# A two-layer sequence model on one core: layer 0's gelu by tanh, the last units' work split between engines, single units routed, and the plan's place

## The chip, the core and the metric

The kernel runs on one core of a Trainium2 chip. A core has five engines, each with its own queue of instructions that it takes strictly in order: TensorE (PE, with weight loads shown as PEld), VectorE (DVE), ScalarE (ACT), GpSimd (POOL) and SyncE (SP, which here only issues transfers). Engines wait for each other by semaphores. The metric is the device time of one execution in microseconds (us). Line numbers (L748) are those of the kernel before.

## The reference, cut to what matters

The input x has 8 sequences of 1024 tokens with 256 features. Two layers follow, each with a post-norm.

```python
# layer 0: feature-wise linear attention, then gelu (the tanh form), then a spectral filter
Q = elu(x@Wq + bq) + 1;  K = elu(x@Wk + bk) + 1;  v = x@Wv + bv
V = Q * sum(K*v, 1) / (Q * sum(K, 1) + 1e-6)
x = layernorm(x + gelu(V@Wo + bo))                  # jax.nn.gelu, approximate
x = layernorm(x + real(ifft(fft(x) @ w)) + bias)
# layer 1: causal softmax attention with 16 heads and a linear position bias
x = layernorm(x + attention(x))
# ... then a block whose attention runs ACROSS the 8 sequences at each position,
#     and a mixture of 8 experts, top 2, 2560 places for each expert
h = x + attn_over_sequences(ln(x)) @ proj.T
p = softmax(ln(h) @ router);  top2 = top_k(p, 2)
# rows of an expert are numbered in token order; rows past its capacity are dropped
moe[token] += gelu_exact(rows @ w1[e]) @ w2[e] * weight
x = layernorm(x + h + moe)
```

## The kernel before, in words

A sequence n is worked through in four steps.

*Layer 0* (`pre(n)`): the sequence is loaded, transposed, multiplied by the three weights, and comes through elu, sums, a reciprocal and the output product. `added` (L725) ends a half layer for four blocks of two tiles each (128 x 512 values): PE's product in PSUM, the bias added by DVE (`shifted`, L736), for the first half the gelu on ACT (L748) and the addition to x on POOL (L753). The blocks' tiles come from a ring of two buffers (`half_row`); elu's tiles from a ring of five (`row`). ACT's functions need tables; those of Exp and of the gelu by tanh are different ones, and a change loads a table.

*Softmax attention* (`run`, L1672 on): for each sequence and each of four head groups 24 steps. A step makes the scores of one piece for the weights (L938, mask L949) with ACT's exponential into `pT` (L952), the scores of the next head group for its row maxima (L872, mask L882) with DVE's maximum (L885), and the value products of an earlier piece (L965). There is one PSUM buffer for each of the two kinds of scores.

*Across sequences* (`across`): in units of two tiles (256 positions, u = 0 to 3 in each sequence), norm, projection, DVE's products of queries and keys (L1223) and their sums over a head (L1239), softmax over the sequences so far (L1255 to L1276), POOL's weighing of the values (`weigh`, L1289, two instructions for each part of two sequences), for the last two sequences gathered by PE (L1338), projection and sum (L1397, L1409), second norm (DVE statistics, POOL root L1079 and L1082, ACT), router product and copy `rt` (L1447).

*Routing* (`dispatch`, L1453 on): for half a sequence, two units at once: softmax, top 2, the rank of each row in its expert (PE L1521 and L1524, DVE L1531), its place, and four fields beside each row (POOL L1599, L1606); then one indirect transfer for each tile and each of the two choices sends 128 rows into the expert-sorted buffer `xg` (L1617): four sends for a unit.

The order of instructions is written out when the kernel is built. Work beside attention is made of tasks, each with an engine and a cost; a planner keeps a clock for each engine, and between the steps it issues those tasks that fit ahead of the next scores (`beside`), or, without attention beside them, the one that can start first (`drain`). `pre(n+2)` is queued in the last head group of sequence n, `across(n-1)` in the first of sequence n. So a changed cost or a changed task may change the order of everything behind it. For the last sequence (n = 7) attention goes by halves of the queries; its units 2 and 3 come after the last attention, with more ring buffers.

Behind that stands the *plan* (L1862 on): DVE computes from the counts of the eight experts which block of 256 rows belongs to which expert, and the indices of the rows to fetch. Then come the *experts*: rows are fetched by POOL's indirect transfers (L2006), run through both products (L2056, gelu L2063, L2070), weighed, normed and put into the output (L2120).

## Time and profile before

| what | value |
|---|---|
| median of 3 runs | 3421.26 us (3418.32 to 3422.33) |
| profiled execution, its own time | 3418.51 us |
| its span, first to last instruction | 3416.8 us |
| PE busy | 3158.0 us (92%) |
| DVE busy | 2163.0 us (63%) |
| ACT busy | 1403.1 us (41%) |
| POOL busy | 1323.3 us (39%) |
| first and last exponential of L952 | about 167 and 2359 us |
| first fetch for the experts (L2006) | 2470.65 us |

The page cuts the span in 40 slices and gives each engine's busy share in tenths. A group's row tells line, engine, operation, output from input, shapes, count, then the busy time, the mean of one in ns, the idle time of the engine just before these instructions and what ended most of it. A row of the stage windows tells the stretch, its length, and for each engine its busy time with the number of instructions, then PE's granted clock, the DMA share and GB/s. A timeline's row tells start, duration, engine, line, operation, and in brackets the idle time before it and what ended it. PE's ends are modelled, so a busy PE need not be PE at its peak.

### The profile page before, as it was taken

The page shows a single profiled execution, that of the slowest core. Times are in us where ns is not written, and L with a number is a line of the kernel's source. Part 1 is how long each engine was busy: PE and PEld are TensorE (multiplying, and loading weights), DVE is VectorE, ACT ScalarE, POOL GpSimd, SP SyncE. Part 2 cuts the span into 40 slices and gives each one's busy share as a digit, 9 for nine tenths or more (in the row PEclk, how much of TensorE's full clock was granted, in tenths as well). Part 3 has the DMA queues.
Part 4 walks back from the last instruction along what each step waited for, and adds up shares of the span by engine and source line. Part 5 has one row for each costly group of instructions (what it writes and reads, how often), then busy time and mean ns, then how long its engine had stood idle before and what let it go on. Part 6 is the DMA issues. An engine that isn't in the chain of part 4 may idle for free. (4 is left out here: it accounts for less than half of the span.)

```text
span 3416.8 us, 51611 instructions
## 1 busy us (share of the span) xinstructions
PE 3158.0 (92%) x19664; PEld 1880.7 (55%) x19664; DVE 2163.0 (63%) x5125; ACT 1403.1 (41%) x2314; POOL 1323.3 (39%) x1671
## 2 busy tenths in 40 slices
PE   6899999999999999998989988998399999999998
PEld 4434435444445434444444434455388888888887
DVE  5666576776776786688688678887534433343443
ACT  3245456565556556456546544444011111111111
POOL 3111012221322222223232323447556666666665
PEclk9999999999999999999999999999699999999999
DMA  2085000010110110111111111232314425334231
GB/s 87 1 155 111 1 21 27 29 35 4 56 44 17 52 40 17 52 40 38 50 35 38 40 50 55 67 118 83 126 55 138 137 63 187 91 112 137 90 116 49
DMA packets 142957, 227.23 MB, mean 67 GB/s; under 512 B 25290, under 2 KB 114452, under 8 KB 139760
## 3 DMA queue, kind: packets, MB, share of 16 engines
q1 hardware_dynamic: 104640, 114.87, 11.9%
q0 software_dynamic: 37248, 108.22, 9.9%
q8 instruction: 156, 2.56, 0.3%
q14 instruction: 97, 0.79, 0.1%
q10 hardware_dynamic: 816, 0.79, 0.1%
HBM read 232.08 MB, written 94.19 MB: 95 GB/s over the span
## 5 line engine op out<-in xcount | busy, mean ns | idle before, releaser
L885 DVE TENSOR_REDUCE mx<-s 128x2 f32<-128x1024 f32 (+3 forms) x768 | 733.5, 955 | 402.6 <-PE s L882 270.8
L952 ACT ACTIVATE pT<-st 128x1024 f32<-128x1024 f32 (+3 forms) x768 | 622.6, 811 | 717.2 <-PE st L949 475.3
L938 PE MATMUL st<-qt,kt 32*128 32x512 f32 (+3 forms) x3072 | 715.7, 542 | 125.1 <-ACT pT L952 115.5
L872 PE MATMUL s<-kt,qt 32*128 32x512 f32 (+3 forms) x3072 | 714.8, 542 | 7.1 <-DVE mx L885 6.1
L938 PEld LDWEIGHTS st<-qt,kt 32*128 32x128 f32 x3072 | 233.6, 186 | 497.3 <-ACT pT L952 351.7
L2063 ACT ACTIVATE hT<-h 128x512 f32<-128x512 f32 x256 | 152.8, 597 | 761.3 <-PE h L2056 761.3
L2056 PE MATMUL h<-xeT,we 128*128 128x256 f32 x2048 | 454.5, 380 | 1.4 <-DVE xeT L1991 1.4
L2070 PE MATMUL y<-we,hT 128*128 128x256 f32 x2048 | 452.5, 379 | 0.0
L2070 PEld LDWEIGHTS y<-we,hT 128*128 128x128 f32 x2048 | 389.1, 190 | 52.9
L2056 PEld LDWEIGHTS h<-xeT,we 128*128 128x128 f32 x2048 | 385.2, 191 | 51.7 <-DVE xeT L1991 1.8
L2090 DVE SCALAR_TENSOR_TENSOR yo<-y,ws,sums 128x256 f32<-128x256 f32 x128 | 61.7, 482 | 464.5 <-DMA sums<-out,row 334.2
L965 PE MATMUL pv<-pT,vv 128*32 128x512 f32 (+3 forms) x3072 | 332.3, 505 | 0.5 <-ACT pT L952 0.5
L872 PEld LDWEIGHTS s<-kt,qt 32*128 32x128 f32 x3072 | 233.2, 185 | 39.4 <-DVE mx L885 33.3
L1005 POOL TENSOR_TENSOR x<-x,ah 128x256 f32<-128x256 f32 x64 | 49.4, 772 | 433.7 <-DVE ah L994 384.6
L1289 POOL TENSOR_TENSOR pa<-v,sc 128x256 f32<-128x256 f32 (+1 forms) x266 | 159.3, 628 | 128.2 <-DVE sc L1276 65.1
L949 PEld LDWEIGHTS <-late_keys 128*128 128x128 bf16 x1024 | 58.3, 97 | 229.2 <-issue 214.2
L2120 POOL DMA_INDIRECT out<-yo,row x128 | 135.0, 1054 | 68.7 <-DVE yo L2111 47.5
L2006 POOL DMA_INDIRECT xin<-xg,idx_x x128 | 134.7, 1053 | 41.3 <-issue 26.2
L949 PE MATMUL st<-ident_h,late_keys 128*128 128x128 bf16 x1024 | 147.3, 226 | 0.0
L1617 POOL DMA_INDIRECT xg<-h,id x128 | 132.5, 1035 | 37.5 <-issue 33.0
L2038 POOL DMA_INDIRECT sums<-out,row x128 | 130.0, 1016 | 43.1 <-issue 38.0
L882 PE MATMUL s<-late_keys,ident_h 128*128 128x128 bf16 x1024 | 143.1, 222 | 0.0
(257 smaller groups left out, 4697.5 us busy)
## 6 DMA issues: line engine op xcount, KB each, us to landing
xg<-zero SPq DMA_DIRECT2D x8, 2610.0 KB, 28.4
x<-in_x SPq DMA_DIRECT2D x8, 1024.0 KB, 13.9
lone<-total SPq DMA_DIRECT2D x64, 128.0 KB, 2.4
xmid<-x SPq DMA_DIRECT2D x6, 1024.0 KB, 4.4
xh<-xmid SPq DMA_DIRECT2D x24, 256.0 KB, 2.7
out<-xh SPq DMA_DIRECT2D x24, 256.0 KB, 2.1
total<-xh SPq DMA_DIRECT2D x24, 256.0 KB, 2.4
we<-in_wexp SPq DMA_DIRECT2D x3, 2048.0 KB, 15.2
```

Of the source, the lines that this page charges most:

```text
L872: nc.tensor.matmul(ps[:, u, :kn], lhsT=qt[r0 : r0 + 32, i * P : (i + 1) * P], rhs=kt[r0 : r0 + 32, k0 : k0 + kn], start=True, stop=not diag,)
L882: nc.tensor.matmul(ps[:, u, kn - P : kn], lhsT=ident_h, rhs=late_keys, start=False, stop=True)
L885: nc.vector.tensor_reduce(out=mxs[g % 2][:, i, 2 * pair : 2 * pair + 2, half], in_=ps[:, :, :kn], axis=AX.X, op=ALU.max,)
L938: nc.tensor.matmul(st[:, u, :w], lhsT=kt[r0 : r0 + 32, kb * P : (kb + 1) * P], rhs=qt[r0 : r0 + 32, q0 + off : q0 + 512], start=True, stop ...
L949: nc.tensor.matmul(st[:, u, :P], lhsT=late_keys, rhs=ident_h, start=False, stop=True)
L952: nc.scalar.activation(pT[:, :, :w], st[:, :, :w], AF.Exp)
L965: nc.tensor.matmul(pv[32 * hh : 32 * hh + 32, off:512], lhsT=vv[:, kb, (4 * g + hh) * VE : (4 * g + hh) * VE + 32], rhs=tiles[hh // 2][:, ...
L1289: nc.gpsimd.tensor_tensor(out=out[:, :, r * P : (r + 1) * P].rearrange("p t (g d) -> p t g d", d=HD), in0=tile[:, t0 : t0 + m, :].rearrang ...
L2056: nc.tensor.matmul(ps[:, f * GS : (f + 1) * GS], lhsT=w1_s[:, c, (f0 + f) * P : (f0 + f + 1) * P], rhs=xeT[:, c, :], start=(c == 0), stop= ...
L2063: nc.scalar.activation(hT[:, f0 : f0 + 2, :], ps.rearrange("p (f g) -> p f g", f=2), AF.Gelu)
L2070: nc.tensor.matmul(ps[:, t * D : (t + 1) * D], lhsT=hT[:, f, t * P : (t + 1) * P], rhs=w2_s[:, f, :], start=(f == 0), stop=(f == FC - 1),)
L2120: put = nc.gpsimd.indirect_dma_start(out=rows_out, out_offset=bass.IndirectOffsetOnAxis(ap=row[:, 1, i : i + 1] if i < GB else idx_l[:, b ...
```

## The change

1. Layer 0's gelu is written out: with g half of the shifted value (the output bias is halved once at the start), ACT makes the square with a scale, DVE (square + c) * g, ACT the tanh of that, DVE (tanh + 1) * g. The tile e comes from the ring of five. The gelu instruction and its table go.
2. For the last sequence's units 2 and 3, the four key products of the unit's second tile are issued on POOL. For unit 3, the weighing of its first tile is issued on DVE.
3. These two units are routed one at a time, each as soon as its router product is there (`lone`), on 2 tiles in place of 4.
4. In the routing the top-2 weights are computed ahead of the ranks, and only the field of the last choice stays behind the places.
5. The plan's block is marked to keep its written order on DVE.

```diff
+ROOT, CUBE = (2 / 3.141592653589793) ** 0.5, 0.044715
...
+    nc.vector.tensor_scalar(out=bo_r, in0=bo_r, scalar1=0.5, scalar2=None, op0=ALU.mult)
...
-                    t = Task("DVE", 0.69, shifted, [t])
-                    ps.readers.append(t)
                     if gelu:
-                        def act(g=g):
-                            nc.scalar.activation(g.get(), g.get(), AF.Gelu_apprx_tanh)
-
-                        t = Task("ACT", 0.65, act, [t], table="gelu")
+                        t = Task("DVE", 0.74, halved, [t])
+                        ps.readers.append(t)
+                        e = row.take(f"{name}e{n}_{j0}")
...
+                        t = Task("ACT", 0.6, square, [t], [e])
+                        t = Task("DVE", 0.72, inner_, [t])
+                        t = Task("ACT", 0.6, tanh, [t], table="exp")
+                        t = Task("DVE", 0.72, outer, [t])
+                        e.readers.append(t)
+                    else:
+                        t = Task("DVE", 0.69, shifted, [t])
+                        ps.readers.append(t)
...
+                        aside = n == N - 1 and u >= 2 and i == 1
...
-                            nc.vector.tensor_tensor(
+                            (nc.gpsimd if aside else nc.vector).tensor_tensor(
                                 out=pr.get()[:, :m, :].rearrange("p t (r e) -> p t r e", r=2),
...
+                        both_do = n == N - 1 and u == 3 and i == 0
...
+                        if both_do:
+                            t = late("DVE", 0.3 + 0.4 * m, part, [shared, *there], [pa])
+                        else:
+                            t = late("POOL", 0.3 + 0.5 * m, part, [shared, *there, *turn_], [pa])
+                            turn_ = [t]
...
-                if u % 2 == 0:
+                lone = n == N - 1 and u >= NB // 2 - 2
+                lo = 0 if lone else 2 * (u % 2)
+                if lo == 0:
                     rt = rtr.take(f"rt{nm}")
...
-                if u % 2:
-                    dispatch(n, u // 2, rt, routed[u // 2])
+                if lone or lo:
+                    dispatch(n, first_block, rt, routed[first_block])
...
             chosen = late("DVE", 1.25, earlier, [t])
...
+            weighed_ = late("DVE", 0.75, weights_, [chosen])
...
-            t = late("DVE", 1.5, weights_, [slots])
+            t = late("DVE", 0.8, which_last, [slots, weighed_])
...
-    with tc.tile_pool(name="plan", bufs=1) as rt:
+    with tc.tile_pool(name="plan", bufs=1) as rt, tc.manual_schedule(engines={nc.vector.engine}):
```

More of the change, by code (lines that the diff above doesn't have):

```diff
@@ L733, in added, with halved @@
                     t = token_tasks(ps, j0 % 4, use[j0 // 4], weight, need, (g,))
+                    def halved(ps=ps, g=g):
+                        nc.vector.scalar_tensor_tensor(
+                            out=g.get().rearrange("p (j d) -> p j d", d=D),
+                            in0=ps.get().rearrange("p (j d) -> p j d", d=D),
+                            scalar=0.5,
+                            in1=bias.unsqueeze(1).to_broadcast([P, 2, D]),
+                            op0=ALU.mult,
+                            op1=ALU.add,
+                        )
                     def shifted(ps=ps, g=g):
@@ L741, in shifted, with square, inner_, tanh @@
                         )
-                    t = Task("DVE", 0.69, shifted, [t])
-                    ps.readers.append(t)
                     if gelu:
-                        def act(g=g):
-                            nc.scalar.activation(g.get(), g.get(), AF.Gelu_apprx_tanh)
-                        t = Task("ACT", 0.65, act, [t], table="gelu")
+                        t = Task("DVE", 0.74, halved, [t])
+                        ps.readers.append(t)
+                        e = row.take(f"{name}e{n}_{j0}")
+                        def square(e=e, g=g):
+                            nc.scalar.activation(
+                                e.get(), g.get(), AF.Square, scale=(8 * ROOT * CUBE) ** 0.5
+                            )
+                        def inner_(e=e, g=g):
+                            nc.vector.scalar_tensor_tensor(
+                                out=e.get(),
+                                in0=e.get(),
+                                scalar=2 * ROOT,
+                                in1=g.get(),
+                                op0=ALU.add,
+                                op1=ALU.mult,
+                            )
+                        def tanh(e=e):
+                            nc.scalar.activation(e.get(), e.get(), AF.Tanh)
+                        def outer(e=e, g=g):
+                            nc.vector.scalar_tensor_tensor(
+                                out=g.get(),
+                                in0=e.get(),
+                                scalar=1.0,
+                                in1=g.get(),
+                                op0=ALU.add,
+                                op1=ALU.mult,
+                            )
+                        t = Task("ACT", 0.6, square, [t], [e])
[6 more added lines that the diff above has]
+                        ps.readers.append(t)
                     def plus(g=g, j0=j0):
@@ L1220, in across, with product @@
                         pr = prr.take(f"pr{nm}_{i}_{t0}")
-                        def product(pr=pr, tile=kv[0], qa=qa, i=i, t0=t0, m=m):
-                            nc.vector.tensor_tensor(
+                        aside = n == N - 1 and u >= 2 and i == 1
+                        def product(pr=pr, tile=kv[0], qa=qa, i=i, t0=t0, m=m, aside=aside):
+                            (nc.gpsimd if aside else nc.vector).tensor_tensor(
                                 out=pr.get()[:, :m, :].rearrange("p t (r e) -> p t r e", r=2),
@@ L1233, in product @@
                             )
-                        t = late("DVE", 0.2 + 0.27 * m, product, there[0] + got, [pr])
+                        t = late(
+                            "POOL" if aside else "DVE",
+                            0.1 + 0.58 * m if aside else 0.2 + 0.27 * m,
+                            product,
+                            there[0] + got,
+                            [pr],
+                        )
                         kv[0].readers.append(t)
@@ L1284, in across, with weigh @@
                 mx.readers.append(shared)
-                def weigh(out, tile, sc, i, t0, m):
+                def weigh(out, tile, sc, i, t0, m, engine=nc.gpsimd):
                     for r in range(2):
-                        nc.gpsimd.tensor_tensor(
+                        engine.tensor_tensor(
                             out=out[:, :, r * P : (r + 1) * P].rearrange(
@@ L1323, in across, with part @@
                         pa = par.take(f"pa{nm}_{i}_{t0}")
-                        def part(pa=pa, tile=tile, sc=sc, i=i, t0=t0, m=m):
-                            weigh(pa.get()[:, :m, :], tile.get(), sc.get(), i, t0, m)
-                        t = late("POOL", 0.3 + 0.5 * m, part, [shared, *there, *turn_], [pa])
-                        turn_ = [t]
+                        both_do = n == N - 1 and u == 3 and i == 0
+                        def part(pa=pa, tile=tile, sc=sc, i=i, t0=t0, m=m, both_do=both_do):
+                            engine = nc.vector if both_do else nc.gpsimd
+                            weigh(pa.get()[:, :m, :], tile.get(), sc.get(), i, t0, m, engine)
+                        if both_do:
[3 more added lines that the diff above has]
+                            turn_ = [t]
                         tile.readers.append(t)
@@ L1444, in across, with out @@
                 rT.readers.append(t)
-                def out(ps=ps, rt=rt, u=u):
+                def out(ps=ps, rt=rt, lo=lo):
                     nc.scalar.copy(
-                        out=rt.get()[:, 0, 2 * (u % 2) : 2 * (u % 2) + 2, :],
+                        out=rt.get()[:, 0, lo : lo + 2, :],
                         in_=ps.get()[:, : 2 * E].rearrange("p (i e) -> p i e", e=E),
@@ L1453, in across, with dispatch @@
                 ps.readers.append(t)
-                routed.setdefault(u // 2, []).append((h, t, normed))
-                if u % 2:
-                    dispatch(n, u // 2, rt, routed[u // 2])
+                first_block = j0 - lo
+                routed.setdefault(first_block, []).append((h, t, normed))
+                if lone or lo:
+                    dispatch(n, first_block, rt, routed[first_block])
         counted = []
-        def dispatch(n, hf, rt, units):
-            nm = f"{n}_{hf}"
+        def dispatch(n, first_block, rt, units):
+            nm, many = f"{n}_{first_block}", 2 * len(units)
             rs, ids = rsr.take(f"rs{nm}"), idr.take(f"id{nm}")
-            part = lambda k: rt.get()[:, k]
-            col = lambda k: rs.get()[:, k]
-            bc = lambda k: col(k).unsqueeze(2).to_broadcast([P, HB, E])
+            part = lambda k: rt.get()[:, k, :many]
+            col = lambda k: rs.get()[:, k, :many]
+            bc = lambda k: col(k).unsqueeze(2).to_broadcast([P, many, E])
             tt = nc.vector.tensor_tensor
@@ L1486, in dispatch @@
             t = late("DVE", 0.65, probs, [t])
-            each = iota_e.unsqueeze(1).to_broadcast([P, HB, E])
+            each = iota_e.unsqueeze(1).to_broadcast([P, many, E])
             def choose(k):
@@ L1510, in earlier @@
                 nc.vector.tensor_copy(out=part(4)[:, :2], in_=part(5)[:, :2])
-                tt(out=part(4)[:, 2:], in0=part(5)[:, 2:], in1=part(5)[:, :-2], op=ALU.add)
+                if many > 2:
+                    tt(out=part(4)[:, 2:], in0=part(5)[:, 2:], in1=part(5)[:, :-2], op=ALU.add)
                 tt(out=part(5), in0=part(4), in1=part(3), op=ALU.subtract)
@@ L1516, in dispatch, with weights_ @@
             flat = lambda k: part(k).rearrange("p j e -> p (j e)")
+            def weights_():
+                tt(out=col(0), in0=col(1), in1=col(2), op=ALU.add)
+                nc.vector.reciprocal(out=col(0), in_=col(0))
+                for k in range(2):
+                    tt(out=col(1 + k), in0=col(1 + k), in1=col(0), op=ALU.mult)
+            weighed_ = late("DVE", 0.75, weights_, [chosen])
             def rank():
-                n_ = HB * E
+                n_ = many * E
                 for lhs, rhs, start in ((before, 3, True), (ones, 5, False)):
@@ L1524, in rank @@
                 nc.tensor.matmul(
-                    ps.get()[:, n_ : n_ + E], lhsT=ones, rhs=part(4)[:, HB - 1], start=True, stop=True
+                    ps.get()[:, n_ : n_ + E], lhsT=ones, rhs=part(4)[:, many - 1], start=True, stop=True
                 )
@@ L1532, in ranked @@
                     out=part(5),
-                    in0=ps.get()[:, : HB * E].rearrange("p (j e) -> p j e", e=E),
-                    in1=counts.unsqueeze(1).to_broadcast([P, HB, E]),
+                    in0=ps.get()[:, : many * E].rearrange("p (j e) -> p j e", e=E),
+                    in1=counts.unsqueeze(1).to_broadcast([P, many, E]),
                     op=ALU.add,
                 )
-                tt(out=counts, in0=counts, in1=ps.get()[:, HB * E : (HB + 1) * E], op=ALU.add)
+                tt(out=counts, in0=counts, in1=ps.get()[:, many * E : (many + 1) * E], op=ALU.add)
             t = first_in("DVE", 0.4, ranked, [t])
@@ L1559, in slot @@
                 nc.vector.scalar_tensor_tensor(
-                    out=ids.get()[:, k],
+                    out=ids.get()[:, k, :many],
                     in0=col(6),
@@ L1570, in dispatch, with which_last @@
             slots = late("DVE", 1.2, lambda: slot(1), [t])
-            def weights_():
-                tt(out=col(0), in0=col(1), in1=col(2), op=ALU.add)
-                nc.vector.reciprocal(out=col(0), in_=col(0))
-                for k in range(2):
-                    tt(out=col(1 + k), in0=col(1 + k), in1=col(0), op=ALU.mult)
+            def which_last():
                 nc.vector.tensor_scalar(
@@ L1583, in weights_ @@
                 nc.vector.tensor_scalar(
-                    out=placed[:, n * NB + HB * hf : n * NB + HB * (hf + 1)],
+                    out=placed[:, n * NB + first_block : n * NB + first_block + many],
                     in0=col(7),
@@ L1596, in fields @@
                 def fields(v=v, h=h):
-                    j0 = HB * hf + 2 * v
+                    j0 = first_block + 2 * v
                     r = h.get()
```

## The prediction

> **What bounds the kernel now.** I read the page's slices first, then stage sums, then groups, then the timeline behind the last attention. The slices (each 85.4 us):

> ```profile
> PE   6899999999999999998989988998399999999998
> ...
> DVE  5666576776776786688688678887534433343443
> ...
> POOL 3111012221322222223232323447556666666665
> ```

> PE is the busy engine everywhere but in two places: the first slices, where layer 0 of the first sequence has nothing beside it, and the slice with the 3 (2392 to 2477), where attention is over and the last units of the second layer are finished one after the other. So the kernel has four stages: start (to 167, the first exponential of L952), attention with filler (to 2360), the hole (to 2471, the first row fetch of L2006), experts (to the end). The change leaves the experts' instructions as they are, so I price the other three. In the attention stage:

> ```profile
> 1000.00:1400.00 400.00, 379.15 (x2688) 180.11 (x2680) 293.15 (x593) 225.98 (x362) 108.39 (x147) 0.98 0.09 29
> ...
> sum 1460.00, PE 1382.03 PEld 635.16 DVE 1071.58 ACT 808.03 POOL 371.68; mean PE 345.51 PEld 158.79 DVE 267.89 ACT 202.01 POOL 92.92
> ```

> Over 340 to 1800 PE is idle for 1460 - 1382 = 78 us (5.3%), DVE is 73% busy, ACT 55%. What PE waits for, from the groups:

> ```profile
> L938 PE MATMUL st<-qt,kt 32*128 32x512 f32 (+3 forms) x3072 | 715.7, 542 | 125.1 <-ACT pT L952 115.5
> L872 PE MATMUL s<-kt,qt 32*128 32x512 f32 (+3 forms) x3072 | 714.8, 542 | 7.1 <-DVE mx L885 6.1
> ```

> Nearly all is waiting for ACT's exponential (there is one score buffer); DVE's maxima hardly ever stop PE.

> **Gelu by tanh: what ACT gives up.**

> ```profile
> L748 ACT ACT_TABLE_LOAD x28 | 35.9, 1283 | 2.7 <-DVE og L736 1.3 <-DVE lna L480 0.9
> L952 ACT ACT_TABLE_LOAD x27 | 34.6, 1283 | 2.6 <-PE st L949 2.1
> ...
> L748 ACT ACTIVATE og<-og 128x512 f32<-128x512 f32 x32 | 20.1, 629 | 14.4 <-DVE og L736 14.0
> ```

> The page's own 58 loads are these 55 and three single ones; in the built order of the changed program two are left (the first, and the experts' Gelu). In the attention stage 54 loads go (27 pairs, 28 blocks of two tiles). A block held ACT for 2 x 1.283 + 0.629 = 3.20 us; now Square and Tanh hold it for 2 x 0.63 = 1.26, in two pieces. That is 28 x 1.94 = 54 us less on ACT, of which only what PE waited for counts. Six windows laid around the loads (46 of the 54):

> ```profile
> 752.50:775.50 23.00, 21.04 (x156) 12.24 (x160) 18.77 (x43) 20.73 (x28) 8.11 (x10) 1.00 0.04 12
> ...
> 1575.00:1608.00 33.00, 24.49 (x182) 12.09 (x178) 23.38 (x58) 24.18 (x32) 18.86 (x26) 0.90 0.06 18
> sum 164.50, PE 135.55 PEld 71.58 DVE 123.54 ACT 130.63 POOL 68.41; mean PE 22.59 PEld 11.93 DVE 20.59 ACT 21.77 POOL 11.40
> ```

> PE idles 28.95 us of 164.5. At the stage's 5.3% it would be 8.8, so 20.2 us belong to 46 loads: 0.44 each, 23.7 for 54. If the idle time shrinks in proportion to ACT's block (1.94 of 3.20), 14.4 come back; if the short pieces disturb nothing, 23.7. I take 19. Outer bounds: 0 (PE's order is limited elsewhere) and 54 (every microsecond of ACT counts).

> [...]

> **What DVE gets.** Per block the shift becomes a scaled shift (taken as 0.05 us more than the 0.68 of L736), and two three-operand instructions on 128x512 come in; the same form at L610 takes 0.68 to 0.71. So 28 x 1.43 = 40 us more in the attention stage. Bounds: 0 (the row L872: PE waited 6.1 us for maxima in the whole run) and 40 (DVE sets the pace). Between: a run of 24 steps lasts some 68 us, so a maximum comes every 2.8 us; each of 56 new instructions of 0.69 us is hit with a chance of 0.25 and then delays it by 0.35, 56 x 0.25 x 0.35 = 5. I take 5, near the row. POOL's additions come later by about 2 us a block; two sequences of lead cover that. If the lead failed, the drain before the next head group would show it. Attention: -19 + 5 = -14.

> **Start: +3.** Here the chain is bare, and the table load (58.2) stood in a wait for the queries' product, so nothing is won by dropping it. The first pair of blocks went DVE 67.51, ACT 68.23, POOL 68.94 to 70.2 and 71.26 to 72.5. Now the second scaled shift (69.83) stands ahead of the first inner product in DVE's order: square to 71.2, products to 72.0, tanh to 72.7, outer to 73.5; POOL's additions end near 74.0 and 75.3, 2.8 later. The second pair is 4.8 later, but its filter rows waited for the first half's statistics anyway. I take +3, between 0 and +6. The halving of bo_r waits for a load issued ahead of own_c's, whose scaling waits anyway.

> **The hole: -6.** DVE's and POOL's rows there:

> ```profile
> 2385.01 1.29 DVE L1223 TENSOR_TENSOR pr<-qa,k 128x512 f32<-128x512 f32 x2 [4.27 <-DMA k<-kvd]
> ...
> 2408.90 2.10 DVE L1223 TENSOR_TENSOR pr<-qa,k 128x512 f32<-128x512 f32 x2
> ...
> 2421.00 0.42 DVE L1276 TENSOR_TENSOR sc<-sc,mx 128x256 f32<-128x256 f32 x1
> ```
> ```profile
> 2405.59 6.46 POOL L1289 TENSOR_TENSOR pa<-v,sc 128x256 f32<-128x256 f32 x8 [2.63 <-issue]
> ...
> 2427.30 5.82 POOL L1289 TENSOR_TENSOR pa<-v,sc 128x256 f32<-128x256 f32 x10
> ```

> DVE works without a pause from 2385 to 2418: 16 products, 16 sums and the routing of the half before. A product takes 0.60 start to start alone (1.29 for two), 1.05 beside POOL (2.10 for two); POOL's weighing 0.58 alone (5.82 for ten), 0.81 in that mixture (6.46 for eight). So POOL and DVE don't add up on such operands. Eight products go to POOL, into its idle stretch 2392 to 2402 (1.2 each, as L1409's 1.18 for the same size): 8 x 0.6 = 4.8 off DVE. Then unit 3's 16 weighings (2421.66 to 2433.1) halve: 8 x 0.58 = 4.6 less on POOL, but the others go at about 0.85: 8 x 0.27 = 2.2 given back. Root L1079 of unit 3 (2439.17) should come 7 us earlier, at 2432.

> [...]

> From that root on the sends count:

> ```profile
> 2439.17 0.23 POOL L1079 TENSOR_SCALAR ln<-ln 128x2 f32<-128x2 f32 x1
> ...
> 2448.16 0.98 POOL L1617 DMA_INDIRECT xg<-h,id  x1 [0.30 <-issue]
> ...
> 2457.36 0.21 POOL L1606 COPY h<-rs 128x8 f32<-128x8 f32 x1 [7.93 <-DVE rs L1580]
> ...
> 2467.44 0.97 POOL L1617 DMA_INDIRECT xg<-h,id  x1 [0.30 <-issue]
> 2470.65 1.10 POOL L2006 DMA_INDIRECT xin<-xg,idx_x  x1 [2.24 <-DMA xg<-h,id]
> ```

> Before, 7 sends follow the root, POOL waits 7.93 us for the routing, 8 follow: 29.2 us to the end of the last. Routing unit 2 alone frees four of the eight, for some 35 more DVE rows of 0.2 us that run while POOL sends. But in the changed order the products stand where eight sends stood (2380.7 to 2391.5; three are left there), and 21 sends now follow the root: 1.0 + 21 x 1.275 + 1.1 for two pairs of field writes = 28.9. The wait is filled with sends, not removed. And the plan doesn't go last: the built order still threads its DVE rows (5.5 us in 2452 to 2458) between the last routing's, so unit 3's fields come near 2453, when POOL gets there too. Moving the weights' four small rows is worth 0.5. So 7 less up to 2 of waiting: -6, between 0 and -12 (no sends piled up).

> **Sum.** +3 - 14 - 6 = -17. The profiled execution took 3418.51 (span 3416.8, 1.7 around it): 3401.5. The runs' median of 3421.26 lies 2.75 higher; I forecast 3404.

> **Rivals.** (1) ACT's relief counts more: every exponential comes sooner, 40 of its 54 us return: -35 - 6 + 3, about 3383. For it: 115.5 us of waits on ACT. Against: only some 29 us lie around the loads. (2) It does little: the idle time around loads was work that PE lacked anyway, and the planner, which writes the whole order anew from its costs, spreads it elsewhere; attention 0, hole -6, start +3: 3418. For it: the 2.3 us steps are full of filler; and the plan not moving is one part that doesn't do what it says. (3) DVE takes ACT's place (slower): in the attention stage it holds 73%, now 76%, and more in runs with routing work (313 of 400 us in 1400 to 1800). If each added DVE microsecond delays a maximum in full, +40 - 19 + 3 - 6 = +18: 3439. It is slower by over 0.2% once the price passes (6.8 + 22) / 40 = 0.72 a microsecond. Against: L872's 6.1 us.

> **Numbers.** Forecast 0.60, (1) 0.10, (2) 0.17, (3) 0.13. A new order of some 670 steps also moves things by several us either way. The range leaves out (3) and the far part of (1): 3386 to 3424. About 0.2% (6.8 us) is what a measurement here can tell: faster 0.70, same 0.17, slower 0.13.

> **What would show it.** Two table loads; in the six gelu regions PE idle near 8%, not 17%; idle before the weights' score matmuls (L938 of before) down by about 20 us, before the maxima's (L872) still under 15; first exponential near 170; hole (last exponential to first row fetch) 105 instead of 111 us, with POOL sending without a pause after the last root. Wrong if DVE's maxima become what ends PE's waits, if the last attention ends no earlier than 2350, or if POOL waits for the routing again.

## The result and the profile after

The changed kernel takes 3394.46 us (median of 6 runs, 3383.54 to 3405.03); the kernel before takes 3421.7 beside it. The ratio is 0.9926, 95% interval 0.991 to 0.9943. The profiled execution took 3396.47 us, its span is 3394.8. Lines are from here on those of the changed kernel: weights' scores L986, maxima's scores L920, exponential L1000, the gelu L764 to L782, cross-sequence products L1274 and their sums L1296, POOL's weighing L1346, root L1127, field writes L1672 and L1679, sends L1690, first row fetch L2079.

Two groups of the page of the changed kernel answer to L938 and L872 of before (busy us, mean ns, then the idle time ahead of them and what ended most of it):

```profile
L986 PE MATMUL st<-qt,kt 32*128 32x512 f32 (+3 forms) x3072 | 714.2, 541 | 110.4 <-ACT pT L1000 100.6
L920 PE MATMUL s<-kt,qt 32*128 32x512 f32 (+3 forms) x3072 | 712.2, 540 | 7.6 <-DVE mx L933 6.8
```

Waiting for ACT's exponential went from 115.5 to 100.6 us (all idle time ahead of that group from 125.1 to 110.4); the maxima still hold PE for under 8 us, with 49 us more work on DVE (2211.9 in all). Windows around the gelus of the attention stage (busy us of each engine with the number of instructions, PE's granted clock, DMA share, GB/s), laid where each kernel has its gelus, first seven of the kernel before, then nine of the changed one:

```profile
527.00:546.00 19.00, 15.74 (x114) 9.06 (x112) 13.87 (x34) 17.04 (x23) 8.87 (x13) 1.00 0.03 8
...
1579.00:1600.00 21.00, 13.55 (x124) 7.90 (x124) 17.57 (x50) 17.12 (x20) 12.21 (x18) 0.95 0.02 8
...
sum 170.00, PE 137.74 PEld 77.42 DVE 135.22 ACT 142.67 POOL 66.85; mean PE 19.68 PEld 11.06 DVE 19.32 ACT 20.38 POOL 9.55
```
```profile
535.00:561.00 26.00, 26.00 (x172) 13.65 (x174) 22.56 (x46) 16.96 (x32) 8.63 (x9) 1.00 0.26 81
...
1560.00:1578.00 18.00, 16.00 (x140) 8.98 (x144) 17.30 (x36) 9.45 (x16) 6.64 (x6) 1.00 0.01 1
...
sum 193.00, PE 183.02 PEld 98.37 DVE 165.66 ACT 122.29 POOL 54.58; mean PE 20.34 PEld 10.93 DVE 18.41 ACT 13.59 POOL 6.06
```

PE was idle for 32.3 of 170 us around the gelus (19%) and is now idle for 10.0 of 193 (5%). The column behind the busy times needs attention too: the 0.95 of 1579 to 1600 comes from a stretch granted 0.50 that begins at 1597.72 and lasts 6.83 us. A pair of score matmuls of 512 columns took 0.70 us ahead of it (1595.23) and 1.22 in it (1599.51).

To follow the time I split each stage into three parts, all from the trace: *idle* (length less PE's busy time), *slow* (half of PE's busy time inside stretches with a granted clock of 0.5) and *work* (the rest). *Slow* is an estimate of what the half clock cost: the score and value matmuls of 512 columns took 1.06 to 1.21 us in such stretches and 0.59 to 0.69 outside them (medians, in four profiles). A sequence n is taken by its 96 exponentials: n=1 to 6 are the exponentials 97 to 672, n=7 the last 96. Attention and hole are parted at the start of the last exponential.

| profile | first exp. | n=1-6: length = idle + slow + work | n=7: length = idle + slow + work | attention | hole | experts |
|---|---|---|---|---|---|---|
| before | 167.5 | 1656.4 = 98.4 + 19.1 + 1538.9 | 294.2 = 25.4 + 12.4 + 256.3 | 2191.9 | 111.2 | 946.1 |
| changed | 168.7 | 1630.5 = 82.8 + 9.7 + 1538.1 | 299.0 = 27.6 + 19.5 + 252.0 | 2167.8 | 115.7 | 942.6 |

So start +1.2, attention -24.1, hole +4.5, experts -3.6: -22.0 of span. In attention idle fell by 16.3, slow by 2.5 (-9.4 in n=1 to 6, +7.1 in n=7), work by 5.4.

### The profile page after: what moved, and what is told of

It reads as the page before. It is cut to its first block, busy times and chain, and to the rows that moved or that the text cites. A ratio compares the mean times of both kernels' runs of the same rounds, so it can differ in the third digit from the quotient of the medians.

```text
span 3394.8 us, 51728 instructions
## 1 busy us (share of the span) xinstructions
PE 3155.3 (93%) x19670; PEld 1882.2 (55%) x19670; DVE 2211.9 (65%) x5232; ACT 1346.2 (40%) x2291; POOL 1330.1 (39%) x1671
## 5 line engine op out<-in xcount | busy, mean ns | idle before, releaser
L1000 ACT ACTIVATE pT<-st 128x1024 f32<-128x1024 f32 (+3 forms) x768 | 622.3, 810 | 743.8 <-PE st L997 498.8
L986 PE MATMUL st<-qt,kt 32*128 32x512 f32 (+3 forms) x3072 | 714.2, 541 | 110.4 <-ACT pT L1000 100.6
L920 PE MATMUL s<-kt,qt 32*128 32x512 f32 (+3 forms) x3072 | 712.2, 540 | 7.6 <-DVE mx L933 6.8
L986 PEld LDWEIGHTS st<-qt,kt 32*128 32x128 f32 x3072 | 233.2, 185 | 484.7 <-ACT pT L1000 330.5
L920 PEld LDWEIGHTS s<-kt,qt 32*128 32x128 f32 x3072 | 232.2, 185 | 41.0 <-DVE mx L933 34.7
L1346 POOL TENSOR_TENSOR pa<-v,sc 128x256 f32<-128x256 f32 (+1 forms) x258 | 155.9, 634 | 104.1 <-DVE sc L1333 60.2
L2079 POOL DMA_INDIRECT xin<-xg,idx_x x128 | 134.2, 1049 | 41.3 <-issue 26.6
L1690 POOL DMA_INDIRECT xg<-h,id x128 | 130.8, 1022 | 34.7 <-issue 32.2
```

Source lines behind the costliest of these rows:

```text
L920: nc.tensor.matmul(ps[:, u, :kn], lhsT=qt[r0 : r0 + 32, i * P : (i + 1) * P], rhs=kt[r0 : r0 + 32, k0 : k0 + kn], start=True, stop=not diag,)
L986: nc.tensor.matmul(st[:, u, :w], lhsT=kt[r0 : r0 + 32, kb * P : (kb + 1) * P], rhs=qt[r0 : r0 + 32, q0 + off : q0 + 512], start=True, stop ...
L1000: nc.scalar.activation(pT[:, :, :w], st[:, :, :w], AF.Exp)
L1346: engine.tensor_tensor(out=out[:, :, r * P : (r + 1) * P].rearrange("p t (g d) -> p t g d", d=HD), in0=tile[:, t0 : t0 + m, :].rearrange(" ...
```

## The experiments

Theory: the recorded sum. A table load costs PE 0.44 us, a microsecond of VectorE 0.125, the two parts add, and the hole is set by the work in it. Rivals: the prices are larger and hide each other; or the order that the planner writes, not the instructions, makes the difference.

The runs fell on four chips: on the first and on the last the kernel before takes 3422 and 3419 us, on the other two 3453. The changed kernel's ratio itself moved with it (0.9926 and 0.9893), so times are compared on chips of one kind, and across the kinds a ratio is good to some 0.003 (11 us).

**Each half of the change alone.** e1 is the kernel before with part 1 of the change and nothing else; e2 is the changed kernel with part 1 taken out, so that parts 2 to 5 remain:

```diff
-                        t = Task("DVE", 0.74, halved, [t])
...
-                        t = Task("ACT", 0.6, square, [t], [e])
-                        t = Task("DVE", 0.72, inner_, [t])
-                        t = Task("ACT", 0.6, tanh, [t], table="exp")
-                        t = Task("DVE", 0.72, outer, [t])
...
+                        t = Task("ACT", 0.65, act, [t], table="gelu")
```

> The kernel before with the gelu by tanh alone; products, weighing, routing and plan of the last units as before. Attention stage is taken from the first to the last exponential (before 2191.9 us, changed kernel 2167.7), the hole from there to the first fetch of expert rows (111.2 and 115.8). Theory (the gain is the table loads'; the shorter attention leaves about 5 us of filler behind; the last units' parts give about nothing): attention 2168, hole 116, whole time 20 to 27 us under before, about that of the changed kernel. Rival (the parts behind attention earn 6 us, as forecast, and the hole hides it): hole 121 to 122, whole time only 14 to 18 under before.

> The changed kernel with the old gelu and its table loads; shared products and weighing, single routing, weights ahead, plan marked. Attention as before, 2192. Theory (the late start in the hole comes from filler that the shorter attention leaves over, not from these parts): hole 111, whole time within 3 us of before. Rival A (these parts are harmful in themselves: products on POOL stop DVE's small instructions, sends pile up): hole 115 to 117, whole time 4 to 6 over before. Rival B (forecast): hole 105, 6 under.

Measured: e1 3417.06, ratio 0.9896 (0.9875 to 0.9918); e2 3459.74, ratio 1.0025 (1.0012 to 1.0038). The gelu is the whole gain (e1 lies 36 us under the kernel before on its chip, where 20 to 27 were expected); the four other parts cost 0.25% by themselves. The attention order of neither is that of before or of the changed kernel beyond the first sequence (the routing's costs, part 4, change the plan), so the two don't add exactly. The holes were 117.7 and 115.2 us: either half lengthens it, so the theory for e2 (111) fell, and its rival A (115 to 117) came true. Parts 2 to 5 were not taken apart further, but for one half of part 2 below.

**The two terms of the attention sum, each put back or doubled.** e3 adds a one-column gelu ahead of each square, so 56 loads return (with each pair of loads 0.2 us of ACT for that gelu); e4 lets a same-sized instruction follow each of the two new ones on DVE. The planner is not told, and the order is that of the changed kernel on PE, DVE and POOL.

```diff
+                            nc.scalar.activation(e.get()[:, :1], g.get()[:, :1], AF.Gelu_apprx_tanh)
                             nc.scalar.activation(
                                 e.get(), g.get(), AF.Square, scale=(8 * ROOT * CUBE) ** 0.5
                             )
```

e4's addition in `inner_`; the one in `outer` does the same on g:

```diff
+                            nc.vector.scalar_tensor_tensor(
+                                out=e.get(),
+                                in0=e.get(),
+                                scalar=1.0,
+                                in1=e.get(),
+                                op0=ALU.mult,
+                                op1=ALU.max,
+                            )
```

> The changed kernel with one more ACT instruction ahead of each square: a gelu of one column of g into e, which the square then overwrites. So each block's table loads come back (56 of them), with 0.2 us of ACT beside them, while every other instruction keeps its place, since the planner is told nothing. Theory (the loads are the gain): 54 loads in the attention stage at 0.35 to 0.45 us each, attention 19 to 26 longer, 2187 to 2194, whole time near before. Rival (the gain came from the new order that the planner wrote, not from the loads): attention under 2176, whole time still 15 or more under before.

> The changed kernel with each of DVE's two new instructions of a block followed by one of the same kind and size (the maximum of a tile with itself, in place), the planner told nothing: 39 us more of DVE in the attention stage in the same order of all else. Theory (forecast's price of 0.125 for each microsecond): attention 5 longer, 2173; bounds 2 and 10. Rival (DVE sets the pace by now, price 0.7 or more): attention 27 or more longer, 2195.

e8 and e9 are the same two with the planner told, and e11 is the changed kernel itself on a chip of that kind:

```diff
-                        t = Task("ACT", 0.6, square, [t], [e])
+                        t = Task("ACT", 0.83, square, [t], [e], table="gelu")
```
```diff
-                        t = Task("DVE", 0.72, inner_, [t])
+                        t = Task("DVE", 1.44, inner_, [t])
...
-                        t = Task("DVE", 0.72, outer, [t])
+                        t = Task("DVE", 1.44, outer, [t])
```

> The changed kernel once more, beside the other three on one chip. Its ratio to the kernel before should be the 0.9926 found at first (0.991 to 0.994); it gives the stage sums that the other three are to be held against.

> As the run that put the table loads back, but the planner is charged for them (0.83 and table gelu for the square, table exp for the tanh) and writes its order for them. Theory that the large price came from an order not made for the loads: 20 to 30 us over the changed kernel. Rival (ScalarE's time is simply on TensorE's path, whatever the order): 50 to 60 us over it, as with the planner untold.

> As the run with each of the two new VectorE instructions done twice (39 us more), but with their cost to the planner doubled too (1.44 for 0.72). Theory that an order made for them hides them: 0 to 8 us over the changed kernel (the recorded price of 0.125 a microsecond gives 5). Rival (VectorE's time is on TensorE's path): some 25 to 35 over it, as with the planner untold.

Measured: changed 3413.87 (ratio 0.9893, 0.9879 to 0.9907), and over it e3 +70 (3483.7), e8 +63 (3476.99), e4 +41 (3454.7), e9 +88 (3502.25). The recorded prices fail. Telling the planner gains 7 us with the loads and loses 48 with DVE's work: e9's rewritten order is bad by itself (first exponential at 182 us instead of 168, first sequence 265 us instead of 238). The split of attention:

| profile | attention = idle + slow + work |
|---|---|
| changed, this kind of chip | 2182.5 = 127.0 + 40.6 + 2014.9 |
| e3 loads back | 2257.2 = 177.6 + 71.3 + 2008.3 |
| e4 DVE twice | 2223.1 = 142.0 + 54.5 + 2026.6 |
| e8 loads told | 2242.7 = 161.7 + 74.8 + 2006.2 |

In e3 each of the 54 loads in the stage (with its half of a one-column gelu) costs 0.94 us of idle time and 0.57 us of half clock. How the second comes about can be seen in consecutive 3.4 us windows of e3:

```profile
1892.60:1896.00 3.40, 3.40 (x27) 1.63 (x27) 2.20 (x5) 3.34 (x7) 0.00 (x0) 1.00 0.03 8
1896.00:1899.41 3.41, 0.78 (x8) 0.42 (x10) 2.94 (x7) 3.36 (x8) 1.27 (x1) 1.00 0.13 38
1899.41:1902.82 3.41, 3.41 (x25) 1.75 (x18) 1.68 (x2) 3.34 (x5) 0.00 (x0) 0.50 0.00 0
1902.82:1906.24 3.42, 3.42 (x24) 2.00 (x23) 2.33 (x5) 2.59 (x4) 0.00 (x0) 1.00 0.00 0
```

and in e3's timeline what stands in the second of them:

```profile
1897.18 1.28 ACT L1001 ACT_TABLE_LOAD   x1
1898.48 0.39 ACT L1001 ACTIVATE pT<-st 128x256 f32<-128x256 f32 x1
1898.88 1.28 ACT L764 ACT_TABLE_LOAD   x1
1898.91 0.19 PEld L987 LDWEIGHTS st<-qt,kt 32*128 32x128 f32 x2 [2.80 <-ACT pT L1001]
```

PE waits 2.8 us for an exponential that stands behind a load; it was busy for 0.78 of that window's 3.41 us, and in the next one it is granted half its clock (0.50) though it has no pause (3.41 of 3.41 us busy). The loads of the kernel before did the same, as two of its windows show:

```profile
1024.28:1027.69 3.41, 1.28 (x16) 0.54 (x12) 2.88 (x5) 2.17 (x3) 2.89 (x4) 1.00 0.00 0
1027.69:1031.10 3.41, 3.41 (x18) 1.38 (x15) 3.09 (x6) 0.60 (x1) 0.00 (x0) 0.50 0.00 0
```

In e4 the groups show the second price, the wait for maxima. The first row is of the changed kernel on that kind of chip (e11), the others are e4's:

```profile
L920 PE MATMUL s<-kt,qt 32*128 32x512 f32 (+3 forms) x3072 | 714.4, 542 | 8.0 <-DVE mx L933 7.2
L1002 PE MATMUL st<-qt,kt 32*128 32x512 f32 (+3 forms) x3072 | 717.1, 543 | 120.4 <-ACT pT L1016 106.2
L936 PE MATMUL s<-kt,qt 32*128 32x512 f32 (+3 forms) x3072 | 715.7, 542 | 14.5 <-DVE mx L949 13.5
```

Only 6.5 of 41 us are there (8.0 to 14.5); 15.0 are idle in all, 13.9 half clock, 11.7 longer PE work. What makes the last I can't say.

**Loads away in the order of before, and the order alone.** e10 is the kernel before with Tanh for Gelu in layer 0 (so the gelu is not computed: the run prices the loads alone) and the planner still charged for loads; f2 is e10 uncharged; f1 is e8 without its loads, the changed kernel with only the charge of e8's diff. f3 is the kernel before once more. The edit of e10, and the one that f2 has besides:

```diff
-                            nc.scalar.activation(g.get(), g.get(), AF.Gelu_apprx_tanh)
+                            nc.scalar.activation(g.get(), g.get(), AF.Tanh)
```
```diff
-                        t = Task("ACT", 0.65, act, [t], table="gelu")
+                        t = Task("ACT", 0.65, act, [t], table="exp")
```

> The kernel before with Tanh in place of Gelu in layer 0 (so the gelu is not computed), the planner still charged for two loads a block: TensorE and VectorE rows in the order of before, 56 table loads gone, 72 us less on ScalarE and nothing added on VectorE. The recorded working (0.44 us of TensorE idle per load): attention 24 us shorter than before, in n=1 to 6 about 20. Rival (a microsecond of ScalarE costs TensorE nearly a microsecond, as putting the loads back under the changed order did, some 57 us): attention 45 to 60 shorter. If the first holds here and the large price there, the old order was hiding the loads because its planner had been told of them.

> The kernel before once more, for its stage sums on the chip that runs the other three. On the chip of its first profile its attention stage took 2192 us, of which TensorE was idle for 136 and lost 38 to half-clock windows. Here, where it takes some 31 us longer, the working theory (TensorE's half clock, set off by idle time in single 3.4 us windows, is what multiplies small delays) expects 10 to 20 us more lost to half clock in attention and as much idle; the rival (the chip is slower throughout) expects the extra spread over the experts as well, some 9 us of it there.

> As the run with Tanh in place of Gelu (the gelu is not computed), but the planner is no longer charged for the loads, so it writes the whole order anew. If the new order is what brought the rest of the gain, this lies 15 to 30 us below that run (3437), near 3410 to 3420. Rival (the rest came from splitting the gelu in short pieces): it stays within 8 us of 3437.

> As the run with the loads back and the planner charged for them (3477), the same order, but the loads themselves are left out. Its distance to that run is the price of 56 loads in an order that was written for them; its distance to the changed kernel (3414) is what such an order costs by itself. If loads are cheap where they were planned for (15 us, as in the order of before) this is near 3462 and the order costs 48; rival (loads cost 55 to 65 wherever they stand): near 3417.

Measured: e10 3437.35, ratio 0.9959 (0.9947 to 0.9971); f2 3378.16, ratio 0.9889 (0.9874 to 0.9904); f1 3417.02, ratio 0.9993 (0.9985 to 1.0002). f3 fell on the faster kind, so its question (what is slower on the other kind) stays open; it repeated every stage of before within 2 us, the hole to 0.1.

- 56 loads less in the order written for them: 0.41%, 14 us (10 to 18), 0.25 us each. Less than recorded, not more.
- That order written anew without the charge: another 24 us less (0.70%, across the two kinds of chip, so 13 to 35).
- The same step with the new gelu: f1 is 22.6 us over the changed kernel on the same kind of chip, with none of the 56 loads in it. Its instructions are those of the changed kernel; only their order differs, and it gives back nearly the whole gain. Attention took 2188.7 against 2167.8: idle +7.7, slow +11.0, work +2.4.

Windows of n=1 to 6 and of n=7, first f1, then the changed kernel:

```profile
405.50:2051.60 1646.10, 1560.05 (x10978) 719.13 (x10976) 1262.70 (x2552) 868.90 (x1468) 445.37 (x611) 0.99 0.11 35
2051.60:2358.40 306.80, 277.04 (x1893) 143.31 (x1890) 248.14 (x551) 138.17 (x256) 148.12 (x218) 0.92 0.23 76
```
```profile
406.90:2037.40 1630.50, 1547.74 (x10970) 713.65 (x10968) 1264.20 (x2554) 866.68 (x1465) 446.88 (x618) 0.99 0.11 36
2037.40:2336.40 299.00, 271.47 (x1900) 141.61 (x1898) 247.59 (x542) 139.03 (x259) 139.96 (x210) 0.93 0.23 75
```

ACT and DVE do the same work in both (868.90 and 866.68, 1262.70 and 1264.20); PE's busy time is 12.3 us longer in n=1 to 6 for the same matmuls, and the half clock accounts for that (23.3 us lost against 9.7).

So in two pairs of orders the one written without the charge was 23 to 24 us better. That the charge did it, and not chance, is not shown: e9's order, written with the right cost, was 48 us worse than e4's, written without it, and e8's was 7 better than e3's. A rewritten order moved these kernels by 7 to 48 us, in either direction.

- What the written-out gelu costs over f2's plain tanh: 3394.5 - 3378.2 = 16 us (13 by the ratios), for 40 us of DVE, 18 us of ACT (28 squares of 0.63) and the other parts of the change (between +9 by e2 and -3 by the changed kernel against e1). So the gelu's extras cost 4 to 19 us, at most 0.5 a microsecond of DVE. This is an estimate: f2's order isn't the changed kernel's, and what that is worth is in it. The next 39 us (e4), in an unchanged order, cost 41, or 1.05 each.

**The hole.** Part 2's first half undone, the order up to the end of attention untouched:

```diff
-                        aside = n == N - 1 and u >= 2 and i == 1
+                        aside = False
```

> The changed kernel with units 2 and 3's second key half of products back on VectorE; the order is the same up to the end of attention. [...] Theory that moving the products buys nothing: the hole 1 to 4 us shorter than the changed kernel's 114. Rival (the recorded step, -4.8 for the products): the hole 4 or more longer than 114.

Measured: 3390.61, ratio 0.9920 (0.9906 to 0.9934), not to be told from the changed kernel; the hole 108.3, shorter by 5.7 than the 114 of the expectation, which had said 1 to 4. Its three parts, by the start of unit 2's first product, unit 3's root and the first fetch:

| profile | last exponential to first product | to the last root | to the first fetch (sends in it) | hole |
|---|---|---|---|---|
| before (and f3, e10 within 0.1) | 25.6 | 54.2 | 31.5 (15) | 111.2 |
| changed | 30.4 | 51.2 | 34.2 (21) | 115.7 |
| changed, other kind of chip | 26.6 | 51.9 | 35.5 (21) | 114.0 |
| e1 gelu only | 32.1 | 54.4 | 31.1 (15) | 117.7 |
| e5 products on DVE | 26.3 | 50.2 | 31.8 (16) | 108.3 |

The first part grows for two reasons. More filler is left when attention ends: unit 0's sum, 3.0 us ahead of the last exponential before, is 6.1 behind it in the changed kernel (first row before, second changed):

```profile
2356.41 0.69 DVE L1397 TENSOR_TENSOR h<-pj,x 128x512 f32<-128x512 f32 x1
2342.49 0.68 DVE L1461 TENSOR_TENSOR h<-pj,x 128x512 f32<-128x512 f32 x1
```

It is not the shorter attention as such that leaves it over: f2, with the shortest (2157.0 us), has that sum 3.0 us ahead again and its first product at 25.6; e1 has it 3.5 behind, e2, with the old gelu, 5.7. The other reason is the clock. The same code takes 30.4 and 26.6 us for this part in its two profiles (e11 second), and the column of the clock tells them apart: a stretch of 17.1 us at half clock stands in the first, one of 3.4 us in the second.

```profile
2336.43:2366.79 30.36, 25.90 (x120) 19.57 (x121) 18.96 (x74) 10.60 (x24) 21.38 (x39) 0.72 0.25 82
2350.12:2376.72 26.60, 21.38 (x123) 16.77 (x124) 18.97 (x74) 10.26 (x24) 21.37 (x39) 0.94 0.23 67
```

With the eight products back on DVE the middle part is not longer but 1.0 to 1.7 shorter, and five sends go ahead of the root again. The reason stands in the changed kernel's timeline, DVE's rows and POOL's:

```profile
2377.13 1.26 DVE L1561 TENSOR_TENSOR rt<-rt,rs 128x32 f32<-128x32 f32 x1
2378.42 0.19 DVE L1562 TENSOR_TENSOR rt<-rt,iota_e 128x32 f32<-128x32 f32 x1
...
2379.87 1.25 DVE L1577 TENSOR_TENSOR rt<-rt 128x24 f32<-128x24 f32 x1
2381.16 1.17 DVE L1578 COPY rt<-rt 128x16 f32<-128x16 f32 x1
```
```profile
2377.08 1.26 POOL L1274 TENSOR_TENSOR pr<-qa,freed 128x512 f32<-128x512 f32 x1 [4.13 <-DVE sc L1296]
2379.79 2.51 POOL L1274 TENSOR_TENSOR pr<-qa,k 128x512 f32<-128x512 f32 x2 [1.45 <-issue]
```

L1561 takes 0.19 us elsewhere (the median of its 34) and 1.26 beside a product on POOL, and ends when the product ends (2378.39 and 2378.34): the small routing rows of units 0 and 1 (128x32: four tiles at once), which stood in this place before the change too, are held up for whole products. The kernel before shows it at a smaller size: its row L1498 took 0.55 us at 2359.61, beside weighings of 0.58, and 0.19 at 2392.37, with POOL idle. And behind the root:

```profile
2418.02 0.23 POOL L1127 TENSOR_SCALAR ln<-ln 128x2 f32<-128x2 f32 x1
...
2433.06 0.20 POOL L1679 COPY h<-rs 128x8 f32<-128x8 f32 x1 [0.96 <-DVE rs L1653]
...
2441.71 0.20 POOL L1679 COPY h<-rs 128x8 f32<-128x8 f32 x1 [1.47 <-DVE rs L1653]
...
2452.18 1.09 POOL L2079 DMA_INDIRECT xin<-xg,idx_x  x1 [2.23 <-DMA xg<-h,id]
```

The 7.93 us wait of before is gone, two short ones are left, and six sends more have taken its place. DVE itself now waits for a send:

```profile
2438.89 0.16 DVE L1636 SCALAR_TENSOR_TENSOR id<-rs 128x2 int32<-128x2 f32 x1 [2.17 <-DMA xg<-h,id]
```

The ring of index buffers (`id`) has two. Unit 3's routing, now by itself, takes the one that units 0 and 1 used, whose last sends stand behind the five that the products pushed back. e11 has the same wait (2.16 us); e5, where those five go ahead of the root, has none there.

## Why the prediction was right, and where it was not

The sign and roughly the time were right (3394 for 3404). The hole's sign was wrong, and attention's gain (24 for 14) came in good part from something that the sum didn't hold. That the total fits is partly luck: attention gave 10 us more than forecast and the hole took 10 us more, and the two errors cancel. Taken from before over e10 and f2 to the changed kernel, the steps are -14 (loads), -24 (order) and +13 to +16 (what the written-out gelu adds, with the rest). By that path loads and new work nearly cancel, and the new order is as large as the whole gain. The steps don't add in every order: put back under the changed order, the loads cost 70.

- **Start, +3:** +1.2 measured (first exponential 168.7).
- **ACT, -19:** the sign was right, and so was roughly the idle time: 22.3 us less around the gelus (32.3 to 10.0), where 14.4 to 23.7 was given. But I charged the whole of it to the loads. e10 takes the loads away and leaves the order: 14 us of the total. The order that the planner writes without the charge is worth 23 (f1) to 24 (f2).
- **The step that failed** is the sentence "A new order of some 670 steps also moves things by several us either way": it moved them by some 23 in the two pairs that bear on this change, more than the loads' 14, and the sum had nothing for it. Rival (2) had named the planner, but as one that eats the gain.
- **DVE, +5:** at the low end of what was found, 4 to 19 for the new gelu's extras; past them it is 1.05 a microsecond. Its sign and that it would not win against the relief were right; rival (3)'s price of 0.72 is passed only by the next 39 us, so it fell for this change but not by a wide margin. L872's 6.1 us, on which I leaned, is no upper price: e4 lost 41 us and that row grew by 6.5.
- **What the sum left out** is the clock. I read PE's idle time, and the column of granted clock beside it (0.90 and 1.00 in the two rows I quoted) I didn't price. Half clock cost 37.6 us in attention before, and 35.1 after: 9.4 less in n=1 to 6, 7.1 more in n=7.
- **Hole, -6:** wrong, +4.5. First product to root was to gain 7, gained 3.0: moving the eight products, taken at -4.8, costs 1.0 to 1.7 (e5); what was gained comes from the other parts. The sends behind the root were counted right (21), but the waits between them and their number make that part 2.7 longer. And the first product comes 1.0 (e11) to 4.8 us later: more filler is left when attention ends, and in the profile with the 4.8 the half clock costs 7.7 us there, where it had cost 2.0 before and costs 1.7 in e11. Both I had at zero. By the prediction's own sign ("wrong ... if POOL waits for the routing again") this part failed: POOL waits twice, 0.96 and 1.47 us.
- **Experts, 0:** 3.6 less, but the same code took between 941 and 948 us in the profiles here.

Why the same loads cost 14 us in the order of before and 27 to 40 in e8's is not settled (e8 and f1 ran on different kinds of chip: the ratios to the kernel before, 1.0072 and 0.9993, give 27, those to the changed kernel, 1.0185 and 1.0066, give 40); and which decision of the planner makes f1's order worse wasn't tried.

## What to carry to other kernels

Where an order is planned from costs, an edit has two prices: what its instructions cost in place, and what the rewritten order is worth; run the edit once with the old charge and once with the new to tell them apart. Don't take a short wait row as the price of more work on an engine: double the work and look. Read the column of granted clock beside the idle time: here waiting was paid twice (in e3 0.94 us of idle time and 0.57 of half clock for a load). And ask of a large elementwise instruction moved to GpSimd what stands beside it and behind it: here it held up VectorE's small ones for its whole length (1.26 us in place of 0.19), and pushed five sends back behind it.

## What the runs showed of the hardware

| window | counted | fourteen profiles of this case | before and changed alone |
|---|---|---|---|
| full clock, PE idle under 15% | half clock next | 1 of 8715 | 0 of 1266 |
| full clock, 15 to 35% | half clock next | 83 of 1504 | 13 of 218 |
| full clock, 35 to 50% | half clock next | 61 of 142 | 6 of 17 |
| full clock, above 50% | half clock next | 104 of 110 | 10 of 11 |
| half clock, over 15% | full clock next | 0 of 340 | 0 of 46 |
| half clock, under 15% | full clock next | 257 of 358 | 30 of 40 |

  In this stretch of the changed kernel the clock stayed down with PE nearly full (21.4 of 23.9 us busy):

```profile
2099.88:2123.77 23.89, 21.41 (x94) 9.17 (x95) 15.04 (x45) 10.00 (x20) 7.24 (x13) 0.50 0.18 59
```

  In these profiles, then, over 1.7 us of waiting in one full-clock window was followed by a half-clock window in 104 of 110 cases (with PE full, an estimated 1.7 us more, half of 3.41), sometimes by several; under 0.5 us in a window was followed by one in 1 of 8715.
- **The clock goes with the spread between runs:** the changed kernel's six runs go from 3383.5 us at a mean clock of 0.978 to 3405.0 at 0.970; 0.008 of 3395 us is 27, and the times lie 21.5 apart.
- **VectorE beside GpSimd:** in the changed kernel L1561's 0.19 us became 1.26 at 2377.13, beside a 128x512 product of 1.26; in the kernel before L1498's 0.19 became 0.55 at 2359.61, beside weighings of 0.58.
